# A graph network of four layers: the gate stage between layers 0 and 1 in a fixed order, its sums in memory

## The chip, the cores and the metric

The kernel runs on one core of a Trainium2 chip, in float32. Five engines take part, each with its own in-order queue of instructions: TensorE (PE; its weight loads are PEld), VectorE (DVE), ScalarE (ACT), GpSimd (POOL) and SyncE (SP, which here only issues DMAs; POOL issues DMAs too). The metric is the device time of one execution in microseconds (us). Before the change it is 2096.28 us, the median of 4 runs (2090.04 to 2102.93).

## The reference, cut to what matters

Eight graphs of 2048 nodes with 64 features go through four layers. Each adds its result to its input `x`. Two layers matter here:

```python
# layer 0, its end: every node mixes two candidates by a gate
pair  = stack([industry, g])                       # two vectors per node
coefs = softmax(tanh(pair @ fcW + fcb) @ av)       # over the two
x1    = x + coefs[0] * industry + coefs[1] * g
# layer 1, its start
h     = relu(layernorm(x1)) @ W                    # 'neighbours'
e     = leaky_relu(s_src[:, None] + s_dst[None])   # s = h @ a
x2    = x1 + elu(softmax(where(adj > 0.5, e)) @ h) # 'attention'
```

A softmax over two is a sigmoid of the difference of the scores, so the kernel computes `x1 = x + g + sigmoid(d) * (industry - g)`, where `sigmoid(d) = (1 + tanh(d / 2)) / 2`.

## The kernel before, in words

Two graphs share the 128 partitions, so there are four pairs p, and each pair's 2048 nodes are cut into four chunks c of 512 columns. All stages follow each other in one unrolled program, and a scheduler orders the instructions of each engine ahead of time by its own model. An instruction that goes through `tc.keep_in_program_order` is pinned: it is issued after the instruction that stands before it in the text on its engine. In the layers after the gate stage all matmuls are pinned (`kit.strict`, lines 711 to 721), other instructions are not.

Up to 437 us layer 0 has left `industry` of each chunk in device memory (`ind_dram`) and `g` of each pair on the chip (`gT`, the buffers `hn`). The second half of that (from 245 us, the "edge" stage, lines 1100 to 1187) also loads 12 of 16 tiles of the adjacency matrix (`aT`, 1 MB each) for layer 1. The last four (`aTl`) take the place of `gT[p]` when pair p is through (`late_tile`).

The **gate stage** (lines 1193 to 1264) runs over 16 chunks, pair by pair. For a chunk, `front` loads `industry` (buffer `iv`, 7 of them), puts it and `g` through `scores` (two matmuls into `pf`, a Tanh of 128x1024, L1206 and L1208), and takes two differences on DVE (L1217 of 128x1024, L1218 of 128x512). `back` runs two chunks behind: it multiplies the difference by `av` (`pd`, L1224), takes a Tanh (`cc`, L1226), does three DVE instructions of 128x512 (L1227 to L1229), of which the last adds `x`, which was loaded for it (`xo`, L1234), and writes the chunk to `x1_dram` with a DMA from POOL's queue (L1230).

Layer 1's first **neighbours** (`neighbour_steps(0)`, a generator) are advanced one or two steps per chunk from chunk 7 on. Per chunk of pair 0 it loads `x1` back from memory (L1302), then mean (PE), subtraction (DVE), Square (ACT), variance (PE), Ln and Exp (ACT), a DVE instruction, eight small matmuls `ph`, and copies to `hS`, `vd`, `sc`. At its end it computes the attention's row factors `R` for the first half of the nodes on the chip: 32 matmuls `pb` and four ACT copies (L1341 to L1346).

The **attention** of layer 1 (`attend`) follows. Its DVE instruction `pt` (L1387) makes the weights from `R` and a tile of the adjacency matrix, and PE multiplies them (`o`, `dn`). Its buffers (`att_pt`, six of 4 KB per partition) are opened once the gate stage's are closed, on the same side of the on-chip memory, so they lie where the small weights of layer 0, the `iv` buffers and part of the `th` buffers were.

Of the kernel before, what the change touches and what calls it, by code (L numbers as in the profile page):

```python
# [8 lines left out]
FP = mybir.dt.float32  # L9
FR = mybir.dt.float32r  # L10
AF = mybir.ActivationFunctionType
OP = mybir.AluOpType
# [4 lines left out]
P = 128  # L17
# [601 lines left out]
LN_EXP = "natural_log_exp_and_others"  # L619


class Kit:


# [124 lines left out]
def layer0(kit, hn, x1_dram, open_early, late_tile, between):  # L749
# [40 lines left out]
    with ExitStack() as sA:  # L790
# [110 lines left out]
        with ExitStack() as s1:  # L901
# [11 lines left out]
            def industry(c):  # L913

                acc = [ps.tile([P, CW], FP, tag=f"acc{p}", name=f"acc{p}") for p in range(NP)]
                ds = sb.tile([P, 2, CW], FR, tag="ds", name="ds")
                for g in range(NT // 2):
                    at = sp.tile([P, 2, CW], FR, tag="at", name="at")
                    nc.gpsimd.dma_start(
                        out=at,  # L920
                        in_=t["adjT"][g * 2 * P : (g + 1) * 2 * P, cols(c)].bitcast(FR).rearrange("(k p) n -> p k n", p=P),
                    )
                    for k in range(2):
                        m = 2 * g + k
                        for p in range(NP):
                            for h in range(2):
                                mm(acc[p], Y[h][:, m, p, :], at[:, k, :], start=m + h == 0, stop=m == NT - 1 and h == 1)  # L927
                        if units:
                            units.pop(0)()

                    if g > 0:
                        nc.vector.tensor_tensor(ds, (was if g == 1 else ds).bitcast(FP), at.bitcast(FP), op=OP.add)
                    was = at
                ev = [sb.tile([P, CW], FP, tag="ev", name="ev", bufs=4) for p in range(NP)]
                for p in range(NP):
                    (nc.scalar.copy if p % 2 else nc.vector.tensor_copy)(ev[p], acc[p])  # L936
                deg = ps.tile([P, CW], FP, tag="ph", name="deg", bufs=2)
                for k in range(2):
                    mm(deg, ones_r, ds[:, k, :], start=k == 0, stop=k == 1)
                rdeg = sb.tile([P, CW], FP, tag="rdeg", name="rdeg", bufs=1)  # L940
                nc.vector.tensor_reduce(bad[:, 3 + c : 4 + c], deg, AX.X, OP.min)
                nc.vector.tensor_scalar(bad[:, 3 + c : 4 + c], bad[:, 3 + c : 4 + c], 0.5, None, op0=OP.is_lt)
                nc.vector.tensor_scalar_max(rdeg, deg, 1.0)
                nc.vector.reciprocal(rdeg, rdeg)
                for p in range(NP):
                    nc.vector.tensor_mul(ev[p], ev[p], rdeg)
                    nc.sync.dma_start(out=ind_dram[p, :, cols(c)], in_=ev[p])
# [152 lines left out]
    with ExitStack() as s0:  # L1100
# [64 lines left out]
                nc.scalar.activation(gT[p][:, i * P : (i + 1) * P], pt[:, p, :], AF.Identity, bias=neg1)  # L1165

        now = begin(0)
        late = None
        for i in range(NT):
            pg = ps.tile([P, B, F], FP, tag="pg", name="pgs")  # L1170
# [16 lines left out]
        late()  # L1187

    sP.close()
    next_ = between(None)  # L1190


    with ExitStack() as s0:
        io = s0.enter_context(tc.tile_pool(name="o_io", bufs=7, reuse_waits="tile"))
        sb = s0.enter_context(tc.tile_pool(name="o_sb", bufs=2, reuse_waits="tile"))
        ps = s0.enter_context(tc.tile_pool(name="o_ps", bufs=2, space=PSUM, reuse_waits="tile"))

        def pinned(ins, first):

            if not first:  # L1200
                tc.keep_in_program_order(ins)

        def scores(v):
            pf = ps.tile([P, 2, CW], FP, tag="pf", name="pf")
            for b2 in range(2):
                pinned(mm(pf[:, b2, :], fcW[half(b2), :], v[half(b2), :], start=True, stop=True), b2 == 0)  # L1206
            th = sb.tile([P, 2, CW], FP, tag="th", name="th_s", bufs=4)
            nc.scalar.activation(th, pf, AF.Tanh, bias=fcb)  # L1208
            return th

        def front(p, c):
            s = cols(c)
            iv = io.tile([P, CW], FP, tag="iv", name="iv")
            nc.sync.dma_start(out=iv, in_=ind_dram[p, :, s])
            gv = gT[p][:, s]
            th = [scores(iv), scores(gv)]
            nc.vector.tensor_sub(th[0], th[0], th[1])  # L1217
            nc.vector.tensor_sub(iv, iv, gv)  # L1218
            return p, s, gv, th[0], iv

        def back(x, p, s, gv, th, df):
            pd = ps.tile([P, CW], FP, tag="pd", name="pd")
            for b2 in range(2):
                pinned(mm(pd[half(b2), :], Av, th[:, b2], start=True, stop=True), b2 == 0)  # L1224
            cc = sb.tile([P, CW], FP, tag="cc", name="cc", bufs=1)
            nc.scalar.activation(cc, pd, AF.Tanh, scale=0.5)  # L1226
            nc.vector.scalar_tensor_tensor(df, cc, 1.0, df, op0=OP.add, op1=OP.mult)  # L1227
            nc.vector.scalar_tensor_tensor(df, df, 0.5, gv, op0=OP.mult, op1=OP.add)
            nc.vector.tensor_add(x, x, df)  # L1229
            nc.gpsimd.dma_start(out=x1_dram[p, :, s], in_=x)  # L1230

        def inputs(p, c):
            x = sb.tile([P, CW], FP, tag="x", name="xo", bufs=5)
            nc.sync.dma_start(out=x, in_=t["xT"][p, :, cols(c)])  # L1234
            return x

        behind, freed, xs = [], [], []

        def finish():
            p, c, rest = behind.pop(0)  # L1240
            back(xs.pop(0), *rest)
            if freed:
                late_tile(freed.pop())
            if c == NCW - 1:
                freed.append(p)

        for p in range(NP):
            for c in range(NCW):
                behind.append((p, c, front(p, c)))
                if len(behind) > 1:  # L1250
                    xs.append(inputs(*behind[-2][0:2]))

                if NCW + 2 < p * NCW + c:
                    next(next_, None)
                if len(behind) > 2:
                    finish()
                if NCW + 2 < p * NCW + c:
                    next(next_, None)
        xs.append(inputs(*behind[-1][0:2]))
        for _ in next_:  # L1260
            pass
        while behind:
            finish()
        late_tile(freed.pop())
    ctx.close()


class Layer1:
# [19 lines left out]
    def neighbour_steps(self, p):  # L1288
# [3 lines left out]
        nc, mm = kit.nc, kit.mm  # L1292
        x1_dram, r_dram = self.x1_dram, self.r_dram

        keep = self.sb2 if p else sb
        sc = sb.tile([P, NT, 4], FP, tag="sc", name="sc", bufs=1)
        vd = keep.tile([P, NT, 2], FP, tag="vd", name="vd", bufs=1 + (p > 0))
        wd = keep.tile([P, NT, 2], FP, tag="wd", name="wd", bufs=1 + (p > 0))
        hS = None
        for c in range(NCW):  # L1300
            x = sb.tile([P, CW], FP, tag="x", name="x1", bufs=1)
# [27 lines left out]
        rs = sb.tile([P, 2, NT], FP, tag="rs", name="rs", bufs=1)  # L1329
        nc.scalar.activation(rs, sc[:, :, 2:4].rearrange("p t b -> p b t"), AF.Exp, scale=-0.8)  # L1330
        pr = ps.tile([2 * NT, P], FP, tag="h", name="pr")
        one = nc.tensor.transpose(pr, rs.rearrange("p b t -> p (b t)"), kit.ident)
        if kit.strict:
            kit.tc.keep_in_program_order(one)
        rr = sb.tile([2 * NT, P], FP, tag="rr", name="rr", bufs=1)
        nc.vector.tensor_copy(rr, pr)
        nc.sync.dma_start(out=r_dram[p].rearrange("b (t n) -> (b t) n", n=P), in_=rr)
        self.first = [self.scores(p, 0, b2) for b2 in range(2)] if p == 0 else None

        for b2, r in enumerate(self.first or ()):  # L1340
            for k in range(2):  # L1341
                pb = ps.tile([P, 4, P], FP, tag=("ln", "h")[k], name="pb1")
                for j in range(4):
                    one = rs[:, b2, 4 * k + j : 4 * k + j + 1]
                    mm(pb[:, j, :], one.to_broadcast([P, P]), kit.ident, start=True, stop=True)
                nc.scalar.copy(r[:, cols(k)], pb.rearrange("p k n -> p (k n)"))  # L1346
        yield hS, vd, wd

    def scores(self, p, hf, b2):

        self.turn += 1
        r = (self.sb2 if self.turn % 3 == 0 else self.R).tile([P, HN], FP, tag="R", name="R", bufs=2 - (self.turn % 3 == 0))
        if p == hf == 0:
            return r
        self.kit.nc.sync.dma_start(out=r, in_=self.r_dram[p, b2 : b2 + 1, cols(hf, HN)].to_broadcast([P, HN]))
        return r

# [57 lines left out]

        return [lambda: total(0), end]

    def run(self, aT, now, following):

# [4 lines left out]
        self.ps2 = l1.enter_context(tc.tile_pool(name="att_ps", bufs=2, space=PSUM, reuse_waits="tile"))  # L1426
        kit.use_ln_exp()
        kit.strict = True
        ends = []
        for p in range(NP):  # L1430
            last = p == NP - 1
            if last:
# [362 lines left out]
def four_layers(  # L1795
# [13 lines left out]
    with ExitStack() as s:  # L1809
# [18 lines left out]
            load(NT - NP + p, low.tile([P, N], FR, tag=f"hn{p}", name=f"aTl{p}"))  # L1828

        def between(_):  # L1830
            one = Layer1(kit, x1)
            ahead.append(one)

            def steps():
                for r in one.neighbour_steps(0):
                    yield
                ahead.append(r)

            return steps()

        layer0(kit, hn, x1, early, late_tile, between)
        later = []
# [2 lines left out]
            later.append(Layers23(kit, x1, x3, out, part, ctx))  # L1845
            return later[0].front(ps)

        ahead[0].run(aT, ahead[1], following)
        later[0].run(aT)
        ps = s.enter_context(tc.tile_pool(name="flag_ps", bufs=1, space=PSUM))  # L1850
        nc.vector.tensor_reduce(kit.bad[:, 0:1], kit.bad, AX.X, OP.add)
# [47 lines left out]
```

## Time and profile before

| what | value |
|---|---|
| median of 4 runs | 2096.28 us |
| the profiled execution | 2092.42 us, span 2090.6 us |
| PE busy | 2016.1 us (96%) |
| DVE, ACT, POOL busy | 1212.3 (58%), 461.6 (22%), 260.1 (12%) us |
| gate stage, first `pf` to first `pt` | 437.72 to 533.33 us |

The profile is a page of one execution: busy time of each engine, the span in 40 slices of 52.3 us with a digit for each engine's busy share and for the clock that TensorE was granted (PEclk), the chain of work that ended last, and the costliest groups of instructions. Other views answer for a stretch of time, a tile or a line: busy times by window, an engine's instructions in order of time, and who waited for whom. In a timeline row, the first number is the start, the second the length of the merged group, both in us, and brackets at the end give the idle time before it and what ended that. Instructions are named by line, operation, out<-in and count. A matmul in float32 shows as two instructions.

### The profile page before, as it was taken

What the parts mean: (1) busy time and instruction counts of PE and PEld (TensorE: products, weight loads), DVE (VectorE), ACT (ScalarE), POOL (GpSimd) and SP (SyncE); (2) the same over time, 40 slices, a digit from 0 to 9 for tenths busy, and PEclk for the clock granted to TensorE, in tenths of its full rate; (3) what the DMA queues carried; (4) which work ended last, traced back from release to release, by engine and by line L of the source; (5) the groups of instructions that cost most, each with busy time, mean ns of one, the idle gap of its engine ahead of it and who ended that gap; (6) DMA issues with size and microseconds to landing.
All of it is one profiled execution on the core that took longest, in us unless ns stands there. A gap on an engine that the chain in (4) does not pass through costs nothing.

```text
span 2090.6 us, 23652 instructions
## 1 busy us (share of the span) xinstructions
PE 2016.1 (96%) x9164; PEld 1153.2 (55%) x9164; DVE 1212.3 (58%) x1906; ACT 461.6 (22%) x863; POOL 260.1 (12%) x384
## 2 busy tenths in 40 slices
PE   7999898988999999999999999999999999999997
PEld 4777655622322222226776457765477755577653
DVE  6677488876888888884223652226642256522355
ACT  4321244456211111112121111211111211112100
POOL 0211054420000000000001110002100012100022
PEclk9999899998999999999999999999999999999999
DMA  5666272145111111213110012101022000121000
GB/s 129 184 194 194 76 255 57 37 133 169 62 41 41 42 41 26 61 31 87 57 41 20 24 28 66 56 11 31 22 61 60 30 21 25 37 66 55 6 15 12
DMA packets 85001, 136.06 MB, mean 65 GB/s; under 512 B 32912, under 2 KB 33168, under 8 KB 82640
## 3 DMA queue, kind: packets, MB, share of 16 engines
q1 hardware_dynamic: 66832, 83.86, 13.8%
q0 software_dynamic: 18048, 50.60, 8.8%
q8 instruction: 74, 1.21, 0.2%
q14 instruction: 47, 0.39, 0.1%
HBM read 103.69 MB, written 30.74 MB: 64 GB/s over the span
## 4 chain that ended last, share of the span: by engine, by line
PE 68%; issue 15%; DVE 6%; POOL 5%; DMA 3%; ACT 2%; SPq 0%; POOLq 0%; DVEq 0%; ACTq 0%
PE acc L713 27%; PE o L713 11%; PE dn L713 6%; PE u L713 6%; PE acc L927 2%; PE mean L713 2%; PE pgs L1155 2%; PE var L713 2%; PE py L713 2%; POOL fold L1780 1%; DVE ex L1153 1%; PE ph L713 1%; POOL ot L1781 1%; POOL mix L1154 1%; POOL ot L1782 1%
## 5 line engine op out<-in xcount | busy, mean ns | idle before, releaser
L713 PE MATMUL acc<-aT,parts 128*128 128x512 f32 x1664 | 456.0, 420 | 0.0
L713 PEld LDWEIGHTS acc<-aT,parts 128*128 128x128 f32 x1664 | 307.8, 188 | 111.8 <-issue 49.4
L1768 DVE TENSOR_TENSOR pr<-u,embf 128x512 f32<-128x512 f32 x256 | 170.7, 687 | 138.9 <-PE u L713 132.2
L1387 DVE SCALAR_TENSOR_TENSOR pt<-R,wd,aT 128x1024 f32<-128x1024 f32 x192 | 236.6, 1279 | 19.3 <-PE dn L713 8.1
L713 PE MATMUL o<-pt,hS 128*64 128x512 f32 x1024 | 237.8, 602 | 5.2 <-DVE pt L1387 5.1
L713 PE MATMUL u<-W3f,y 64*128 64x512 f32 x1024 | 241.0, 589 | 0.0
L713 PEld LDWEIGHTS u<-W3f,y 64*128 64x128 f32 x1024 | 99.2, 187 | 120.6 <-issue 120.6
L713 PEld LDWEIGHTS o<-pt,hS 128*64 128x64 f32 x1024 | 68.4, 137 | 165.0 <-issue 150.7
L713 PE MATMUL u<-W3f,v 64*128 64x512 f32 x512 | 138.8, 619 | 0.0
L927 PE MATMUL acc<-at,Y 128*128 128x512 f32 x512 | 134.9, 408 | 1.9 <-DVE ev L936 1.9
L713 PE MATMUL dn<-pt,vd 128*32 128x512 f32 x1024 | 123.1, 598 | 0.0
L1604 DVE TENSOR_TENSOR yb<-py,cb_f 128x512 f32<-128x512 f32 x32 | 22.1, 691 | 173.8 <-PE py L713 173.8
L1780 POOL TENSOR_TENSOR fold<-fold 128x256 f32<-128x256 f32 x64 | 47.7, 745 | 548.5 <-DVE fold L1779 510.6
L927 PEld LDWEIGHTS acc<-at,Y 128*128 128x128 f32 x512 | 93.9, 192 | 24.9 <-issue 4.2
L713 PE MATMUL acc<-aTl,parts 128*128 128x512 f32 x384 | 103.1, 405 | 0.0
L1772 DVE TENSOR_TENSOR pr<-pr 128x512 f32<-128x512 f32 x128 | 88.1, 688 | 2.2
L1387 DVE SCALAR_TENSOR_TENSOR pt<-R,wd,aTl 128x1024 f32<-128x1024 f32 x64 | 79.8, 1282 | 11.4 <-PE dn L713 8.2
L713 PEld LDWEIGHTS acc<-aTl,parts 128*128 128x128 f32 x384 | 72.2, 188 | 21.5 <-issue 5.7
L1155 PE MATMUL pgs<-mix,S 128*128 128x512 f32 x128 | 69.7, 635 | 12.8 <-POOL mix L1154 12.3
L1754 ACT COPY xs<-px 128x128 f32<-128x128 f32 x64 | 17.1, 267 | 272.7 <-POOL ot L1782 210.3
L1154 POOL TENSOR_TENSOR mix<-ex,wt 128x512 f32<-128x512 f32 x64 | 66.6, 1042 | 74.0 <-DVE ex L1153 64.0
L1672 POOL TENSOR_TENSOR bq<-bq,xp 128x512 f32<-128x512 f32 x16 | 20.5, 1283 | 434.1 <-DVE xp L1670 395.6
(307 smaller groups left out, 2711.0 us busy)
## 6 DMA issues: line engine op xcount, KB each, us to landing
at<-in_adjT POOLq DMA_DIRECT2D x32, 512.0 KB, 4.6
raw<-in_adjT SPq DMA_DIRECT2D x64, 256.0 KB, 3.4
aT<-in_adjT POOLq DMA_DIRECT2D x12, 1024.0 KB, 7.0
xp<-xd SPq DMA_DIRECT2D x45, 256.0 KB, 3.0
R<-r_dram SPq DMA_DIRECT2D x14, 512.0 KB, 3.9
hi_dram<-hi SPq DMA_DIRECT2D x16, 264.0 KB, 2.8
lo_dram<-lo SPq DMA_DIRECT2D x16, 264.0 KB, 3.4
hhi<-hi_dram POOLq DMA_DIRECT2D x16, 264.0 KB, 3.1
```

The costliest lines, as they stand in the source:

```text
L713: one = self.nc.tensor.matmul(*args, **kw)
L927: mm(acc[p], Y[h][:, m, p, :], at[:, k, :], start=m + h == 0, stop=m == NT - 1 and h == 1)
L1153: nc.vector.scalar_tensor_tensor(ex, mix, 1.0, ex, op0=OP.max, op1=OP.min)
L1154: nc.gpsimd.tensor_tensor(mix, ex, wt[:, k, :, None].to_broadcast([P, B, F]), op=OP.mult)
L1155: return lambda: mm(flat(pg), S[:, k, :], flat(mix), start=k == 0, stop=k == NB - 1)
L1387: nc.vector.scalar_tensor_tensor(pt, R[b2], wd[:, m, b2 : b2 + 1], aT[m][:, s].bitcast(FP), op0=OP.max, op1=OP.mult)
L1604: nc.vector.tensor_tensor(yb, py, bias[:, None, :].to_broadcast([P, 4, P]), op=OP.add)
L1768: nc.vector.tensor_tensor(a, u[h], emb[:, i, 8 * w : 8 * w + 8, None].to_broadcast([P, 8, F]), op=OP.mult)
L1772: nc.vector.tensor_add(pr[h], pr[h], a)
L1780: nc.gpsimd.tensor_add(fold[:, :, 0:2, :], fold[:, :, 0:2, :], fold[:, :, 2:4, :])
L1781: nc.gpsimd.tensor_add(ot, fold[:, :, 0, :], fold[:, :, 1, :])
L1782: nc.gpsimd.tensor_add(ot, ot, xs)
```

## The change

The gate stage is rewritten. Order: almost every instruction of PE, ACT and DVE in it goes through `keep_in_program_order` (the class `InOrder` does it for DVE and ACT), so the three engines run the text's order; DMAs stay free. Residual: `x` of pairs 1 to 3 is copied from the input to `x1_dram` by SP (1 MB each, memory to memory), issued in the text at the edge stage's start; `g` of these pairs is added to it by three adding DMAs of 1 MB from POOL's queue, and each chunk's own part by an adding DMA of 256 KB, instead of two DVE instructions, the load of `x` and the plain write. Pair 0 keeps its two additions and is written by SP. The factor 1/2 moves into `rdeg` (the industry is stored halved, its Tanh scales by 2). Neighbours: a new generator takes `x1` of pair 0 from the chip (`xs`, four buffers), two chunks at a time; `R` is no longer made on the chip but read back from memory as for later pairs, by two more loads of `R`.

```diff
-                nc.vector.tensor_scalar_max(rdeg, deg, 1.0)
+                nc.vector.tensor_scalar(rdeg, deg, 1.0, 2.0, op0=OP.max, op1=OP.mult)
...
         now = begin(0)
+        for p in range(1, NP):
+            nc.sync.dma_start(out=x1_dram[p], in_=t["xT"][p])
...
+        def scores(v, f):
+            act = A if kit.strict else nc.scalar
             pf = ps.tile([P, 2, CW], FP, tag="pf", name="pf")
             for b2 in range(2):
+                kit.strict = kit.strict or b2 == 1
+                mm(pf[:, b2, :], fcW[half(b2), :], v[half(b2), :], start=True, stop=True)
             th = sb.tile([P, 2, CW], FP, tag="th", name="th_s", bufs=4)
+            act.activation(th, pf, AF.Tanh, bias=fcb, scale=f)
+        def first(i):
+            p, c = chunks[i]
+            iv = ivs[i] = io.tile([P, CW], FP, tag="iv", name="iv")
+            nc.sync.dma_start(out=iv, in_=ind_dram[p, :, cols(c)])
+            ths[i] = scores(iv, 2.0)
+        def second(i):
+            p, c = chunks[i]
+            tgs[i] = scores(gT[p][:, cols(c)], 1.0)
+            V.scalar_tensor_tensor(ivs[i], gT[p][:, cols(c)], -0.5, ivs[i], op0=OP.mult, op1=OP.add)
+        def differ(i):
+            V.tensor_sub(ths[i], ths[i], tgs.pop(i))
+        def third(i):
+            for b2 in range(2):
+                mm(pd[half(b2), :], Av, th[:, b2], start=True, stop=True)
+            A.activation(ccs[i], pd, AF.Tanh, scale=0.5)
+        def fourth(i):
+            V.scalar_tensor_tensor(df, ccs.pop(i), 1.0, df, op0=OP.add, op1=OP.mult)
+            if p:
+                nc.gpsimd.dma_start(out=x1_dram[p, :, cols(c)], in_=df, accum_op=OP.add)
+            else:
+                V.tensor_add(df, df, gT[p][:, cols(c)])
+                V.tensor_add(xs[c], xs[c], df)
+                nc.sync.dma_start(out=x1_dram[p, :, cols(c)], in_=xs[c])
             if c == NCW - 1:
+                late_tile(p)
...
+        for p in range(1, NP):
+            nc.gpsimd.dma_start(out=x1_dram[p], in_=gT[p], accum_op=OP.add)
+        steps = one.first_neighbours(xs, V, A)
+        for i in range(len(chunks)):
+            if i > 2:
+                next(steps, None)
+            if 0 < i < len(chunks) - 1:
+                first(i + 1)
+            third(i)
+            if i + 1 < len(chunks):
+                second(i + 1)
+            fourth(i)
+            if i > 2:
+                next(steps, None)
+            if i + 1 < len(chunks):
+                differ(i + 1)
...
+    def first_neighbours(self, xs, V, A):
+        for d in (0, 2):
+            for k in range(2):
+                mm(mean, kit.avg, xs[d + k], start=True, stop=True)
+                V.tensor_sub(xc[k], xs[d + k], mean)
+                A.activation(q[k], xc[k], AF.Square)
+            yield
+            yield
+            for k in range(2):
+                mm(var[k], kit.avg, q[k], start=True, stop=True)
+            for k in range(2):
+                A.activation(q[k], var[k], AF.Ln, bias=kit.eps)
+            for k in range(2):
+                A.activation(q[k], q[k], AF.Exp, scale=-0.5)
+            yield
+            for k in range(2):
+                V.scalar_tensor_tensor(xc[k], xc[k], 0.0, q[k], op0=OP.max, op1=OP.mult)
+            yield
...
```

What is left out at the end: for each of the two chunks a step with the eight `ph` matmuls and two small Exp, and a step with the copies; then `wd` and `rs`, the transpose `pr`, the write of the row factors and the two loads of `R`. In `neighbour_steps`, now used for pairs 1 to 3 only, the on-chip `R` and its 32 matmuls are gone.

## The prediction, as put on record

> **What bounds it now.** The page has PE at 96% of the span, but only the gate stage changes, so I read that stage. First the windows by stage (columns: window, length, then busy us of PE, PEld, DVE, ACT and POOL, granted clock, DMA share, GB/s):
>
> ```profile
> 437.00:450.00 13.00, 12.64 (x44) 4.30 (x42) 6.57 (x8) 9.63 (x13) 0.00 (x0) 0.77 0.54 161
> 450.00:463.00 13.00, 12.24 (x48) 3.46 (x46) 12.86 (x19) 10.22 (x12) 2.24 (x5) 1.00 0.56 165
> 463.00:486.00 23.00, 15.00 (x34) 4.39 (x32) 11.01 (x17) 9.41 (x12) 1.61 (x3) 0.73 0.61 193
> 486.00:523.00 37.00, 33.78 (x116) 11.83 (x116) 29.72 (x52) 30.38 (x41) 4.33 (x8) 0.98 0.52 171
> 523.00:534.00 11.00, 7.61 (x43) 4.44 (x39) 8.64 (x14) 6.34 (x11) 2.29 (x5) 1.00 0.29 101
> ```
>
> Three regimes: DVE full (450 to 463), a hole with no engine full (463 to 486), then PE, DVE and ACT all near 0.8 to 0.9. What the hole is, the chain of waits says:
>
> ```profile
> 462.99 9.25 DMA xd<-xo
> ...
> 472.67 4.75 DMA x<-xd
> 477.42 0.14 issue
> 477.56 2.04 PE mean L713 x2
> ```
>
> The chunk of `x1` goes to memory behind a 1 MB `aTl` load and comes back, and PE, whose order is fixed, waits at `mean`. The end (523 to 534) is a third loss: `pb` and the copies to `R` stand before the first `pt` at 533.33. So the stage takes 95.6 us (437.72 to 533.33), and no engine is its bound throughout.
>
> **What goes.** DVE: for 12 chunks two of four 128x512 instructions, 24 of 0.69 (L1228, L1229) = 16.5 us. ACT: loads of the function table fall from 8 to 4 of 1.28 = 5.1 us; four copies to `R`, 2.3. PE: 32 `pb`, 4.0. The round trip of `x1` (14 us of chain) goes. SP loses 12 `xo` and 4 `x1` loads, POOL 16 writes. These are large, but they count only as far as the new order lets the engines use them.
>
> **What the order costs.** In the text, chunk i runs: `pd(i)`, second scores of i+1, its Tanh, the difference of i+1 on DVE, and only then `pd(i+1)`. On PE `pd(i+1)` stands ahead of the next second scores, so this is a loop, one round per chunk, with no chunk of slack; before, `back` ran two chunks behind. The links, from these rows (start, length in us):
>
> ```profile
> 450.32 1.13 PE L1206 MATMUL pf<-iv,fcWf 64*128 64x512 f32 x4
> 451.29 1.02 PE L1206 MATMUL pf<-hn,fcWf 64*128 64x512 f32 x4
> 451.50 2.38 ACT L1208 ACTIVATE th_s<-pf,fcbf 128x1024 f32<-128x1024 f32 x2 [0.32 <-PE pf L1206]
> ...
> 495.65 1.10 ACT L1208 ACTIVATE th_s<-pf,fcbf 128x1024 f32<-128x1024 f32 x1
> 496.79 1.23 DVE L1217 TENSOR_TENSOR th_s<-th_s 128x1024 f32<-128x1024 f32 x1 [0.31 <-ACT th_s L1208]
> ```
>
> A four-matmul group holds PE for 1.0 us; from the start of a `pf` group to its Tanh are 1.18 (450.32 to 451.50), the Tanh lasts 1.10, the difference starts 0.04 later and lasts 1.22, and a hop from DVE to PE is 0.1 (`gn` ends 436.56, `ptg` starts 436.70). Round: 1.0 + 1.18 + 1.1 + 0.04 + 1.22 + 0.1 = **4.64 us**. The first scores of the next chunk fit into its gap of 1.6. Before, groups of three (two `pf`, one `pd`) came every 2.93 us, then 3.66 once DVE was full: the order costs more than DVE did.
>
> - Pair 0 keeps three DVE instructions after `cc`, ahead of the difference: 1.2 (`pd` to `cc`) + 0.6 + 3 x 0.7 + 1.22 + 0.15 = 5.27 per round.
> - Start: the first three score groups run at half clock as now (437.72, 439.59, 441.29); the third is now `g`'s, so its Tanh starts at 443.2, the difference ends 445.5, `pd(0)` starts at 445.6.
> - 15 rounds: 4 x 5.27 + 11 x 4.64 = 72.1.
> - A round with two means: difference 1.22, two subtractions 1.32, last Square 0.63, Tanh 1.11, `cc` 0.6, Tanh 1.11 = 6.0, so +1.4; twice, 2.8.
> - A round with two Ln: ACT runs table load, two Ln, load, two Exp, then Tanh, `cc`, Tanh: 2 x 1.28 + 2 x 0.69 + 2 x 0.62 + 1.11 + 0.6 + 1.11 = 8.0, and DVE puts `df` and two 0.66 instructions ahead of the difference, 8.9: +4.3; twice, 8.6.
> - Four rounds with copies (0.16 + 0.41 twice on DVE, of which 0.9 fits in a gap): +0.25 each, 1.0.
> - End after `pd(15)` starts: 1.2 + 0.6 + 0.7 = 2.5.
>
> 445.6 + 72.1 + 2.8 + 8.6 + 1.0 + 2.5 = 532.6 against the 533.4 at which `xo` now ends. **At full clock the order gives back all that was saved.**
>
> **The clock.** Windows around the start of the stage (same columns):
>
> ```profile
> 430.00:435.00 5.00, 2.75 (x4) 0.80 (x4) 2.27 (x3) 0.72 (x1) 2.08 (x2) 0.76 0.16 59
> 435.00:440.00 5.00, 4.12 (x11) 1.90 (x12) 0.85 (x2) 1.29 (x5) 0.00 (x0) 0.50 0.53 157
> 440.00:445.00 5.00, 4.64 (x16) 1.35 (x12) 2.37 (x3) 3.91 (x4) 0.00 (x0) 0.71 0.86 260
> 445.00:450.00 5.00, 5.00 (x24) 1.39 (x20) 4.05 (x5) 4.42 (x6) 0.00 (x0) 1.00 0.01 5
> ```
>
> PE idled for 0.59 and 2.19 us (428 to 432), then the clock is halved until PE has been full for some us. At 5 us windows of 3.0 to 3.7 busy the clock held (65:70, 245:250), so a normal round, 3.0 of 4.64, should hold. In each Ln round PE waits some 3.2 us (two `var`, `pf`, `pd`, `pf` are through 5.1 us into it; `ph` needs the first of DVE's two instructions: 6.9 for `cc`, + 0.7 + 0.7 = 8.3), and at the start PE waits for the first difference. Estimate: after an Ln round a group each of `ph` (1.3), `pf`, `pd` (1.0 each) runs at half clock, up to +3.3, I take 2.8, twice; 1.0 at the start: **+6.6**. Bounds: 0, and half clock in all rounds, +2.0 each, about +26 more.
>
> The Trainium skill ("TensorE: Matmul & The Clock Gate", section "Why this matters for your kernels") only warns of idle gaps over about 3 us between bursts. The row disagrees: 2.19 us was the longest gap before this fall. By the rule the start would cost nothing and the Ln gaps are on its edge, so the stage could end at 532.6; by the row it is 6.6 later.
>
> **The rest.** The three 1 MB copies by SP stand near 250 us, beside `aT` loads. The edge stage had PE busy 45.15 of 50 us at DMA share 0.73 (250:300) and 45.00 at 0.23 (350:400), so it hides DMA: 0, at most +3. An adding DMA of 512 KB took 5.6 us to landing (`xd<-e`) and 0.84 of POOL. Three of 1 MB from 439 are two such each: some 30 us, over before pair 1's attention input is read. Behind them on POOL's queue stand only the chunks' adds and `aTl`; aTl's last use begins 37 us after the stage (570.53). The `iv` buffer is now held until its add has landed, but seven buffers at 4.64 give 28 us. The two `R` loads (3.9) follow the neighbours' last step, chunk 11, four rounds before the end: hidden. Halving in `rdeg`: same instruction, 0. What is open is the first `pt`: its buffers lie where the last `iv` were. Free at once: -2.8 (PE need not wait from the last `pd` to the first `pt`); after the last add: 0.84 + 5.6 = +6.4. I take +1, since only some of six buffers are held.
>
> **Sum.** -0.8 + 6.6 + 1.0 = +6.8 on the profiled execution, 2092.4 to 2099.2. That execution lies 3.9 under the median, so 2096.3 + 6.8 = **2103 us**. A change under 0.5% (10.5 us) is about what this measurement can't tell from none.
>
> **Rivals.**
> 1. *The loop isn't closed, the fullest engine sets the pace.* PE: 16 x 3.0 + 4 x (2.1 + 1.3) = 62, with start and end (7.9 + 2.5) 72 instead of 95.6: -23, 2073. For it: all three engines lose work, PE had 0.94 in 450:463. Against: the text above. Chance 0.15.
> 2. *Full clock, and free `pt` instructions fill DVE's gaps before the end.* -0.8 - 2.8: 2093, 0.10.
> 3. *Slower: the clock doesn't come back.* Place: the gaps of the strict loop; price +2.0 per round beyond those counted. From two further rounds on it is over +10.5; with half of the rounds, +13 to 16 more: 2118. For it: 480:485 still had 0.50 with PE at 5.00. Against: at half clock PE is 6.0 of 6.7 full. Chance 0.22.
> 4. *Attention's start waits for the last adding DMA*: +5.4 over the forecast, 2108.5, 0.13.
>
> That the change doesn't do what it says can only be so in part, as DMAs are free to move.
>
> **Chances.** Forecast 0.40, rivals 0.15, 0.10, 0.22, 0.13. Faster by over 0.5%: rival 1 and 0.02 of the others, 0.17. Slower: rival 3, most of 4, a part of the forecast's own spread, 0.37. Between: 0.46. Range: rival 1 (0.15) and rival 3's far end are left out, 2084 to 2121.
>
> **What would show it.** Right: between 450 and 530 no engine over 0.8 busy; `pd` every 4.6 to 5.3 us, with two rounds of some 9; PE's waits ended by the difference (L1217's successor), clock under 1 after each Ln; no wait of `mean` for a DMA. Wrong: `pd` every 3 to 3.7 us (rival 1), or clock 0.5 through most of the stage (3), or PE idle over 4 us at the first `o` (4). A stage end before 520 would refute the loop.

## The result, and the profile after

The kernel after takes **2100.26 us** (median of 52 runs, 2093.73 to 2111.23) against 2095.71 (78 runs of the kernel before, 2086.8 to 2104.4): a ratio of 1.0027, with a 95% interval of 1.0019 to 1.0035. The two medians by themselves are 4.55 us apart; the differences below go by the ratios, so it is slower by 5.7 us (0.0027 x 2095.7), less than 0.5%. The forecast was +6.8. The profiled execution took 2099.19 us with a span of 2097.4. PE is busy for 2010.3 us (before 2016.1), DVE for 1198.4 (1212.3), ACT for 455.8 (461.6): all three do less, and the time is longer.

From here on, "the stage" is the time from the first `pf` to the first `o` in one trace: 96.95 us before (437.72 to 534.67), **102.30** after (436.70 to 539.00), so +5.35. In the kernel's new text the pinned DVE and ACT instructions all have line L630 (the helper `InOrder`), pinned matmuls L726, `pt` L1465, a chunk's adding DMA L1258, the 1 MB ones L1275.

The windows by stage of the kernel after, in the same stretches and columns as those of before:

```profile
437.00:450.00 13.00, 9.82 (x24) 2.88 (x22) 5.51 (x7) 6.65 (x10) 2.67 (x3) 0.67 0.87 171
450.00:463.00 13.00, 10.54 (x32) 2.76 (x32) 9.36 (x14) 5.54 (x8) 0.00 (x0) 0.87 0.71 191
463.00:486.00 23.00, 17.50 (x62) 6.47 (x60) 11.73 (x19) 15.63 (x22) 2.28 (x3) 0.85 0.46 103
486.00:523.00 37.00, 28.33 (x103) 9.81 (x101) 20.80 (x36) 23.77 (x33) 6.22 (x8) 0.91 0.66 135
523.00:534.00 11.00, 5.52 (x22) 1.39 (x20) 6.09 (x7) 6.12 (x7) 3.11 (x4) 1.00 0.72 150
```

From 450 on no engine is over 0.81 busy, and in the last stretch PE, DVE and ACT are all near half: nothing is full, so something waits in a circle. The chain of waits shows the circle in a plain round (start, length, what):

```profile
515.78 1.08 PE pd L726 x4
516.86 1.08 PE pf L726 x4
...
517.96 1.12 ACT th_s L630
...
519.11 1.24 DVE th_s L630
...
520.39 1.08 PE pd L726 x4
```

`pd`, second scores, Tanh, difference, next `pd`: 4.61 us, five times in a row, against 4.64 predicted. A round with Ln in it, from the same view:

```profile
466.04 1.28 ACT L630
...
467.34 1.27 ACT q L630 x2
...
469.92 1.15 ACT q L630 x2
471.06 1.00 ACT th_s L630
472.07 0.50 ACT cc L630
...
472.59 0.69 DVE iv L630
473.28 0.61 DVE xc L630
...
474.03 2.10 PE ph L726 x8
476.12 2.01 PE pf L726 x4
478.13 1.78 PE pd L726 x4
```

ACT loads a table, makes two Ln, loads again, makes two Exp; the text then sends a Tanh and `cc` through ACT and `df` through DVE before DVE may make `xc`, for which PE waits. And `ph`, `pf` and `pd` then take twice their length, which the windows confirm (column 8 is the granted clock):

```profile
475.00:480.00 5.00, 5.00 (x16) 1.81 (x16) 1.31 (x2) 1.53 (x4) 0.00 (x0) 0.54 0.54 68
480.00:485.00 5.00, 4.13 (x22) 1.64 (x20) 3.42 (x7) 2.94 (x5) 0.87 (x1) 1.00 0.36 67
```

At the end, DVE's rows in order of time:

```profile
536.88 0.69 DVE L630 SCALAR_TENSOR_TENSOR iv<-cc,iv 128x512 f32<-128x512 f32 x1 [2.71 <-ACT cc L630]
537.57 3.67 DVE L1465 SCALAR_TENSOR_TENSOR pt<-R,wd,aT 128x1024 f32<-128x1024 f32 x3
543.92 3.68 DVE L1465 SCALAR_TENSOR_TENSOR pt<-R,wd,aT 128x1024 f32<-128x1024 f32 x3 [2.68 <-DMA xd<-iv]
```

The first three `pt` start at once; the fourth waits 2.68 us for an adding DMA, because, as the trace's releaser and e5_swap below say, its buffer lies on an `iv` buffer that the DMA still reads.

### The profile page after: what moved, and what is told of

It reads as the page before. It is cut to its first block, busy times and chain, and to the rows that moved or that the text cites. A ratio compares the mean times of both kernels' runs of the same rounds, so it can differ in the third digit from the quotient of the medians.

```text
span 2097.4 us, 23519 instructions
## 1 busy us (share of the span) xinstructions
PE 2010.3 (96%) x9132; PEld 1150.8 (55%) x9132; DVE 1198.4 (57%) x1882; ACT 455.8 (22%) x855; POOL 264.7 (13%) x383
## 4 chain that ended last, share of the span: by engine, by line
PE 68%; issue 15%; DVE 6%; POOL 5%; ACT 2%; DMA 2%; POOLq 0%; DVEq 0%; SPq 0%; ACTq 0%
PE acc L726 27%; PE o L726 11%; PE dn L726 6%; PE u L726 6%; PE acc L940 2%; PE pgs L1169 2%; PE mean L726 2%; PE var L726 2%; PE py L726 2%; POOL fold L1858 1%; DVE ex L1167 1%; PE pf L726 1%; PE ph L726 1%; POOL ot L1859 1%; POOL ot L1860 1%
## 5 line engine op out<-in xcount | busy, mean ns | idle before, releaser
L726 PE MATMUL acc<-aT,parts 128*128 128x512 f32 x1664 | 455.7, 419 | 0.0
L726 PEld LDWEIGHTS acc<-aT,parts 128*128 128x128 f32 x1664 | 307.7, 188 | 111.7 <-issue 49.4
L1465 DVE SCALAR_TENSOR_TENSOR pt<-R,wd,aT 128x1024 f32<-128x1024 f32 x192 | 236.5, 1279 | 20.6 <-PE dn L726 6.6
L726 PE MATMUL o<-pt,hS 128*64 128x512 f32 x1024 | 238.2, 602 | 4.3 <-DVE pt L1465 4.1
L726 PE MATMUL u<-W3f,y 64*128 64x512 f32 x1024 | 241.0, 589 | 0.0
L726 PEld LDWEIGHTS u<-W3f,y 64*128 64x128 f32 x1024 | 99.2, 187 | 120.6 <-issue 120.6
L726 PEld LDWEIGHTS o<-pt,hS 128*64 128x64 f32 x1024 | 68.6, 137 | 164.6 <-issue 154.5
L726 PE MATMUL u<-W3f,v 64*128 64x512 f32 x512 | 138.8, 619 | 0.0
L726 PE MATMUL dn<-pt,vd 128*32 128x512 f32 x1024 | 123.1, 598 | 0.0
L726 PE MATMUL acc<-aTl,parts 128*128 128x512 f32 x384 | 103.2, 405 | 0.0
L1465 DVE SCALAR_TENSOR_TENSOR pt<-R,wd,aTl 128x1024 f32<-128x1024 f32 x64 | 79.8, 1281 | 11.4 <-PE dn L726 8.2
L726 PEld LDWEIGHTS acc<-aTl,parts 128*128 128x128 f32 x384 | 72.2, 188 | 21.6 <-issue 5.7
```

Source lines behind the costliest of these rows:

```text
L726: one = self.nc.tensor.matmul(*args, **kw)
L1465: nc.vector.scalar_tensor_tensor(pt, R[b2], wd[:, m, b2 : b2 + 1], aT[m][:, s].bitcast(FP), op0=OP.max, op1=OP.mult)
```

## The experiments

All ratios are against the kernel before, measured beside the kernel on the same chip. "Stage" is from each kernel's own trace. "Plain round" is the distance of `pd` in rounds that hold no work of the neighbours. The profiled execution of e1_slack was its fastest (2095.81 us), that of e5_swap its slowest (2099.24).

| kernel | what differs | stage, us | plain round, us | ratio (95% interval) |
|---|---|---|---|---|
| before | | 96.95 | 2.92 to 3.49 | 1 |
| after | | 102.30 | 4.61 | 1.0027 (1.0019 to 1.0035) |
| e1_slack | a chunk of slack in the text | 102.32 | 2.93 | 1.0058 (1.0041 to 1.0076) |
| e2_free | order left to the scheduler | 85.40 | 4.60 | 0.9959 (0.994 to 0.9978) |
| e3_fill | PE's gaps filled | 94.19 | 4.61 | 0.9998 (0.9986 to 1.0009) |
| e4_dve_sum | residual undone | 114.87 | 5.09 to 6.27 | 1.01 (1.0083 to 1.0116) |
| e5_swap | e1, `pt` not on `iv` | 97.95 | 2.93 | 1.0008 (0.9993 to 1.0023) |
| e6_memory | neighbours undone | 122.50 | 4.61 | 1.0121 (1.0101 to 1.014) |
| e7_free_dve | e2, residual undone | 86.87 | 2.07 to 5.73 | 0.9955 (0.9942 to 0.9969) |
| e8_early | e5, `xc` earlier | 76.74 | 2.93 | 0.9915 (0.9896 to 0.9933) |
| e9_early_dve | e8, residual undone | 87.42 | 3.8 | 0.9964 (0.995 to 0.9977) |
| e10_early_fill | e8, gaps filled | 74.77 | 2.93 | 0.9906 (0.9883 to 0.9928) |
| e11_sooner | e10, neighbours one chunk sooner | 77.20 | 2.93 | 0.9915 (0.99 to 0.9929) |

The time that lies outside the stage (median less stage) is 1998.8 us before, 1998.0 after, and between 1996.3 and 1999.8 in every other row but e1_slack (2002.9). So, to within some 3 us, the stage is where every one of these edits acts.

**e1_slack.** Does the order close the loop?

```diff
-            third(i)
             if i + 1 < len(chunks):
                 second(i + 1)
-            fourth(i)
-            if i > 2:
-                next(steps, None)
+            third(i)
             if i + 1 < len(chunks):
                 differ(i + 1)
+            fourth(i)
+            if i > 2:
+                next(steps, None)
```

> One move in the text: the second scores of chunk i+1 stand before pd of chunk i, and its difference before fourth of chunk i. Theory (the strict order closes a loop of 4.6 us, second scores, Tanh, difference, pd): the loop now has a chunk of slack, pd comes every 3.0 to 3.3 us in plain rounds, every 4.1 in pair 0 (DVE: 1.22 + 4 x 0.69), rounds with two Ln take some 8 (ACT's own work). Stage from first pf to first o 78 us instead of 102; time 2075 us (2070 to 2082). Rival (DMA traffic or buffers that come free late set the pace, the order only happens to fit it): rounds stay above 4.3, time 2093 or more.

Measured: 1.0058, 3 permille above the change. The loop did open; the matmuls of its last chunks, and then the first `o`:

```profile
517.36 1.08 PE L726 MATMUL pd<-th_s,Avf 128*64 128x512 f32 x4
...
520.29 1.08 PE L726 MATMUL pd<-th_s,Avf 128*64 128x512 f32 x4
...
523.22 1.08 PE L726 MATMUL pd<-th_s,Avf 128*64 128x512 f32 x4
525.91 1.08 PE L726 MATMUL pd<-th_s,Avf 128*64 128x512 f32 x4 [1.61 <-DVE th_s L630]
537.09 3.87 PE L726 MATMUL o<-pt,hS 128*64 128x512 f32 x8 [10.10 <-DVE pt L1465]
```

2.93 us per chunk, PE without a gap up to the last `pd`, and then 10.10 us of nothing. So the closed loop is shown, but its rate alone was not worth the 25 us expected: the stage is as long as before. Two other places took it back: the rounds with Ln grew from 9.67 and 10.30 to 13.92 and 11.82 us, and the first `pt`, which came at once in the change, waited:

```profile
526.75 8.67 DMA xd<-iv
...
535.65 1.29 DVE pt L1465
```

The adding DMA was issued at 526.75 on POOL's queue, 2.1 us after a 1 MB load of `aTl` (524.69), and landed 8.67 us later. That is rival 4 of the prediction, in full size, in a kernel that reaches the place sooner.

**e5_swap.** The same with the two pools in the other order, so that `pt` lies on `th`, `cc` and `x`:

```diff
-        io = s0.enter_context(tc.tile_pool(name="o_io", bufs=7, reuse_waits="tile"))
         sb = s0.enter_context(tc.tile_pool(name="o_sb", bufs=2, reuse_waits="tile"))
+        io = s0.enter_context(tc.tile_pool(name="o_io", bufs=7, reuse_waits="tile"))
```

> e1_slack with two lines changed places: the pool of th, cc and x is opened before the pool of iv, so that the attention's pt buffers lie over th, cc and x and not over the iv buffers, which the adding DMAs hold. Theory (e1_slack opened the loop, and the first pt then waited 7.3 us for an adding DMA, more in its timed runs): pt starts within 2 us of the last pd, first o at 529 to 530 in the trace instead of 537.1, time 2087 (2083 to 2091). Rival (e1_slack loses its time by DMA traffic in the whole stage, and the wait at its end is only where it shows): 2096 or more.

Measured: 1.0008, 10 us below e1_slack (0.0050 x 2094) but less than expected. In its trace the wait is gone (last `pd` 535.41, first `pt` 537.77), and the stage is only 4.4 us shorter, because its two rounds around the first Ln were 0.63 and 1.62 us longer than in e1_slack, with both `pf` at half clock, and its first `pd` came 1.13 us later after the stage's start. The rest of the 10 us lies outside the stage, in e1_slack's 2002.9. The rounds with Ln, 14.55 and 11.45 us, are now by far the longest.

**e8_early.** The neighbours' second step goes ahead of the next difference and of `fourth`:

```diff
             third(i)
+            if i > 2:
+                next(steps, None)
             if i + 1 < len(chunks):
                 differ(i + 1)
             fourth(i)
-            if i > 2:
-                next(steps, None)
```

> e5_swap with the second step of the neighbours ahead of the next difference and of fourth in the text (as it stands in the change). Theory (in e1_slack ph waited 7.7 and 5.8 us because DVE's instruction for xc stood behind the difference and fourth, and these behind two Tanh and cc on ACT): ph comes 3 us earlier in each Ln round, the clock falls less: 2080 (2075 to 2085). Rival (the Ln round is ACT's own 8 us, wherever xc stands): within 2 us of e5_swap.

Measured: 0.9915, 2075.82 us, inside the expectation. PE's rows around the first Ln, e1_slack and then e8_early:

```profile
458.41 1.08 PE L726 MATMUL pd<-th_s,Avf 128*64 128x512 f32 x4
467.21 2.10 PE L726 MATMUL ph<-W1x,xc 128*128 128x132 f32 x8 [7.72 <-DVE xc L630]
```

```profile
468.62 1.08 PE L726 MATMUL pd<-th_s,Avf 128*64 128x512 f32 x4
473.06 1.17 PE L726 MATMUL ph<-W1x,xc 128*128 128x132 f32 x8 [3.37 <-DVE xc L630]
```

The wait for `xc` falls from 7.72 to 3.37 us. Against e5_swap, whose waits for `xc` are the same 7.72 and 5.77 us as in e1_slack, the place of one step in the text was worth 19 us (0.0093 x 2092). This kernel is faster than the one before and the one after, and computes the same. DVE's rows at the end of its stage:

```profile
519.68 0.69 DVE L630 SCALAR_TENSOR_TENSOR iv<-cc,iv 128x512 f32<-128x512 f32 x1 [1.21 <-ACT cc L630]
520.29 1.28 DVE L1465 SCALAR_TENSOR_TENSOR pt<-R,wd,aT 128x1024 f32<-128x1024 f32 x1
521.74 3.68 DVE L1465 SCALAR_TENSOR_TENSOR pt<-R,wd,aT 128x1024 f32<-128x1024 f32 x3 [0.17 <-DMA R<-r_dram]
```

The first `pt` follows straight behind the last `fourth`, and the first `o` (521.71) behind this `pt`. Only the second `pt` waits for its half of R, whose load took 8.06 us, and DVE loses no more than 0.17 us by it.

**e2_free.** Order of DVE and ACT free; of the gate's matmuls only the second of each pair pinned; the rest of the change stays.

```diff
-    V, A = InOrder(tc, nc.vector), InOrder(tc, nc.scalar)
+    V, A = nc.vector, nc.scalar
...
-    mm = kit.mm
+    def mm(*args, **kw):
+        one = nc.tensor.matmul(*args, **kw)
+        if pair.pop():
+            tc.keep_in_program_order(one)
+
+    pair = [True, False] * 100
```

> Order of the gate stage left to the scheduler again: DVE and ACT free, and of the gate's matmuls only the second of each pair pinned, as before the change; neighbours' matmuls stay pinned, residual and neighbours as in the change. Theory: rounds without a neighbours' matmul gain slack and fall toward 3.5, rounds with one keep theirs; 5 to 12 us less, 2088 to 2095. Rival (order not at fault): 2098 to 2102, rounds unchanged.

Measured: 0.9959, 14 us below the change (0.0068 x 2094), where 5 to 12 were expected: the change's residual and neighbours with the scheduler's order are faster than the kernel before. The reason in the expectation was wrong: the plain rounds stayed at 4.60, since the scheduler kept `pd` ahead of the second half of the second scores there, for which the Tanh waits. The rounds with neighbours shrank: the nine from `pd(2)` to `pd(11)` take 44.9 us (457.39 to 502.26) against 60.3 (455.46 to 515.78). DVE's rows of e2_free show why:

```profile
469.23 1.29 DVE L1398 SCALAR_TENSOR_TENSOR xc<-xc,q 128x512 f32<-128x512 f32 x2 [1.65 <-ACT q L1395]
471.24 0.69 DVE L1261 SCALAR_TENSOR_TENSOR iv<-cc,iv 128x512 f32<-128x512 f32 x1 [0.71 <-ACT cc L1256]
```

`xc` stands ahead of `df` and starts as soon as its Exp is there. `ph` then waits 0.80 and 1.82 us instead of 3.50 and 4.12, and the clock does not fall in either Ln round.

**e3_fill.** What does the clock cost? Matmuls whose result is overwritten fill PE's gaps, for example:

```diff
             th = ths.pop(i)
+            for k in range(8 if i == 15 else 4 if i < 4 else 0):
+                mm(pd[:, 0:P], kit.ident, kit.ident, start=True, stop=True)
```

and in the same way 16 ahead of the first `ph` after each Ln, and 8 ahead of the first `o`.

> Extra matmuls whose results are overwritten fill PE's gaps: 4 ahead of pd in chunks 0 to 3, 8 ahead of the last pd, 16 ahead of the first ph after each Ln, 8 ahead of the first o. Nothing else changes. Theory (half clock after the gaps costs some 6 to 8 us on the path): granted clock stays 1 after both Ln rounds and at the first o, ph x8 takes 1.1 instead of 2.1, the round after it 4.6 to 5 instead of 5.9, o x8 2.4 shorter; time 2092 to 2095. Rival (the clock falls beside the path, the Ln rounds are long by ACT and DVE alone): no more than 2 us less, or some us more where the fill itself delays pd.

Measured: 0.9998, 6.1 us below the change (0.0029 x 2094), inside the expectation. PE's rows around the first Ln:

```profile
471.88 3.84 PE L726 MATMUL ph<-ident_f 128*128 128x128 f32 x32
475.56 1.07 PE L726 MATMUL ph<-W1x,xc 128*128 128x132 f32 x8
476.55 1.13 PE L726 MATMUL pf<-iv,fcWf 64*128 64x512 f32 x4
477.61 1.08 PE L726 MATMUL pd<-th_s,Avf 128*64 128x512 f32 x4
```

`ph` takes 1.07 instead of 2.10, `pf` 1.13 for 2.08, `pd` 1.08 for 1.82, with more work on PE and not less. From `pd(0)` to `pd(15)` this kernel needs 82.4 us, the change 89.6: 7.2 us.

**e4_dve_sum.** Only the residual undone.

```diff
-            if p:
-                nc.gpsimd.dma_start(out=x1_dram[p, :, cols(c)], in_=df, accum_op=OP.add)
-            else:
-                V.tensor_add(df, df, gT[p][:, cols(c)])
-                V.tensor_add(xs[c], xs[c], df)
-                nc.sync.dma_start(out=x1_dram[p, :, cols(c)], in_=xs[c])
+            x = xs[c] if p == 0 else more.pop(i)
+            V.tensor_add(df, df, gT[p][:, cols(c)])
+            V.tensor_add(x, x, df)
+            (nc.gpsimd if p else nc.sync).dma_start(out=x1_dram[p, :, cols(c)], in_=x)
```

> Only the residual undone: no copies of x in memory, no adding DMAs; pairs 1 to 3 load x, add g and x with two DVE instructions per chunk and write plainly, as pair 0 does. Order and neighbours as in the change. Theory: the two additions stand ahead of the next difference on DVE and lengthen the loop by 0.5 to 0.7 in 12 rounds, 1.4 at the end: 2107 to 2110. Rival (memory traffic of the adding DMAs costs time elsewhere, or the first pt waits for them): the same as the change or up to 3 us faster, 2097 to 2101.

Measured: 1.01, 15 us above the change (0.0073 x 2094), where 7 to 10 were expected: the last five rounds are 5.90, 5.71, 5.09, 6.27 and 5.09 us, 1.0 over 4.61 in the mean, not 0.5 to 0.7. In the chain of waits the two additions stand in the loop, and a longer gap on PE halves the clock (`pd` 1.80 and `pf` 2.02):

```profile
534.29 0.70 DVE iv L630
...
535.62 1.23 DVE th_s L630
...
536.89 1.80 PE pd L726 x4
538.69 2.02 PE pf L726 x4
```

**e7_free_dve** and **e9_early_dve** undo the residual in the same way in two other orders: in that of e2_free, and in that of e8_early.

> e2_free with the residual undone as in e4_dve_sum (x loaded, g and x added by DVE in all pairs, plain writes). Theory (the additions cost only because they stand in the strict loop; 0.6 per round there): against e2_free 4 to 8 us more, 2089 to 2093, the last pt no longer held by an adding DMA (-3). Rival (the residual in memory is worth as much in any order as the 14 us between the change and e4_dve_sum): 2097 or more.

> e8_early with the residual undone as in e4_dve_sum. The two additions were worth 14 us in the strict loop of the change and nothing (2084.0 against 2084.7 us) in the scheduler's order. Theory (DVE paces where the order has slack: 1.22 + 4 x 0.69 = 4.0 per chunk against PE's 2.93): plain rounds 4.0 to 4.1, 8 to 12 us more than e8_early, 2084 to 2088. Rival (the adding DMAs' traffic takes as much back): within 3 us of e8_early.

Measured: e7_free_dve has 0.9955 against 0.9959 of e2_free, no difference, and both numbers of its expectation missed. e9_early_dve has 0.9964 against 0.9915 of e8_early, 10 us, as expected. Its plain rounds are 3.8 us where e8_early has 2.93, with DVE busy for 19.66 of the 20 us from 500: there DVE is what paces. A further 2.46 us is a wait of its last addition for the load of `x`. In e7_free_dve the rounds alternate (2.79, 5.73, 2.07, 5.55), 16.1 us for four where e2_free needs 18.4: the scheduler made another order of it, so this pair compares two orders as well as two residuals. The same edit is worth 15, 0 or 10 us, by the order it stands in.

e7_free_dve shows one thing more. What it keeps of the change is the neighbours by the chip and the text in which they stand; the sums in memory and the pinned DVE and ACT are gone. It is 9 us below the kernel before (0.0045 x 2092). So what the change won in the scheduler's order came with the neighbours and their text, not with the residual.

**e6_memory.** Only the neighbours undone: `x1` of pair 0 read back, one chunk at a time, by the generator of the later pairs.

```diff
-        steps = one.first_neighbours(xs, V, A)
+        steps = one.from_memory()
...
+    def from_memory(self):
+        for r in self.neighbour_steps(0):
+            yield
+        self.first = [self.scores(0, 0, b2) for b2 in range(2)]
+        self.now = r
```

> Only the neighbours undone: the gate stage in the strict order and with the adding DMAs, but x1 of pair 0 read back from memory, one chunk at a time, by the generator of the later pairs (its DVE and ACT instructions not pinned), R still read back. Theory (two chunks at a time make two rounds of 10 us, out of the strict order they would not): four Ln rounds of 6 to 8 us in place of two of 10, clock falls less, 2092 to 2101. Rival (the way by the chip is what keeps the stage as short as it is, the round trip of x1 comes back as in the kernel before): 2105 or more.

Measured: 1.0121, 20 us above the change (0.0094 x 2092). The theory's 2092 to 2101 missed; the rival's number (2105 or more) came, but its reason only in small part. PE's rows:

```profile
461.06 2.08 PE L726 MATMUL mean<-x,avg_f 128*128 128x512 f32 x2 [3.88 <-DMA x<-xd]
...
485.23 1.12 PE L726 MATMUL var<-q,avg_f 128*128 128x512 f32 x2
491.28 1.22 PE L726 MATMUL ph<-W1x,xc 128*128 128x132 f32 x4 [4.92 <-DVE xc L754]
```

Only one `mean` waits for the memory (3.88 us). The rest is that in this generator `ph` follows straight behind `var` on PE, so that the whole way over Ln, Exp and `xc` lies open, four times (4.83 to 4.92 us). This run therefore does not tell what the way by the chip is worth; it points to what the empty steps of the new generator, which put `pf`, `pd` and `pf` between `var` and `ph`, are worth, but does not separate them from the rest that differs (one chunk at a time, DVE and ACT not pinned).

**e10_early_fill** and **e11_sooner.** e8_early with 10 filling matmuls ahead of the first `ph` after each Ln, 5 ahead of the last `pd`, 8 ahead of the first `o`; and this with the neighbours begun one chunk sooner.

```diff
+                    for j in range(10 if k == g == 0 else 0):
+                        mm(ph[:, 0, 0:P], kit.ident, kit.ident, start=True, stop=True)
```

```diff
-            if i > 2:
+            if i > 1:
```

> e8_early with extra matmuls whose results are overwritten: 10 ahead of the first ph after each Ln, 5 ahead of the last pd, 8 ahead of the first o. Theory (half clock costs what its share of the work costs): ph, pf and o that ran at half clock at 474 to 478, 495 to 499 and 522 to 526 run at full clock, 3 to 5 us less, 2071 to 2073. Rival (the waits behind, for R and ACT, take it up): within 1.5 us of e8_early.

> e10_early_fill with the neighbours' steps begun one chunk earlier (i > 1 for i > 2). In e8_early the first o waited for R, whose way through memory took 5.4 and 8.1 us after the neighbours' end. Theory: R is there 3 us earlier, first pt straight after the last fourth; 1 to 3 us less than e10_early_fill. Rival (the mean then waits for the x1 of chunk 1, and the round where DVE is full takes it back): the same or more.

Measured: 2074.57 and 2076.04 us beside 2075.82 of e8_early; the intervals overlap, and neither is told apart from it. In the traces the fill shortens the stage by 2.0 us and the clock no longer falls after its start. In e11_sooner no `pt` waits for R any more. But the first `o` had not waited for R, as the expectation says it did: the second `pt` had, for 0.17 us in e8_early and 0.47 in e10_early_fill, so there was little to win; and the round with the first means takes 9.34 us instead of 4.86, as the rival said.

**e12_slack_again.** e1_slack once more.

> e1_slack once more, one look: its trace (first pf to first o 102.3 us, as in the change) does not account for a median 5 us above the change. Theory (the first pt's wait for the adding DMA varies and was short in that trace): the wait is 12 us or more in this trace, the time 2100 or more. Rival (the time goes elsewhere): the same wait of 7 to 8 us at a time over 2100.

Measured: 2107.22 us, stage 101.93, first `pt` again held for 7.28 us. The theory falls and its rival holds: the time is not in the stage. The first `pf` starts at 444.72 here and at 434.77 in e1_slack, 10 us apart in two executions of one kernel. Half of this is there by 40 us (a DMA that POOL issues at 37.70 in e1_slack comes at 42.55 here); the other half comes between 255 and 273 (POOL's `mix`, 254.93 against 260.37, and a few instructions on 262.94 against 272.98). A row from the first place and the window around the second, e1_slack and then e12_slack_again:

```profile
24.09 3.78 PE L857 MATMUL pr<-tri,MT 64*128 64x64 f32 x32 [1.33 <-DVE Y L905]
...
260.00:280.00 20.00, 17.13 (x78) 11.20 (x78) 17.50 (x27) 8.69 (x19) 11.38 (x15) 1.00 0.74 257
```

```profile
26.13 6.38 PE L857 MATMUL pr<-tri,MT 64*128 64x64 f32 x32 [1.34 <-DVE Y L905]
...
260.00:280.00 20.00, 17.67 (x66) 11.76 (x65) 12.68 (x19) 6.46 (x16) 9.27 (x12) 0.77 0.60 199
```

The same 32 matmul rows take 6.38 us for 3.78, and around 270 PE is as busy at a clock of 0.77 for 1.00 and does 66 rows instead of 78. So the clock is behind the 10 us between these two executions. It does not explain why e1_slack's median stands 3 us over its stage plus 2000; that stays open, and since the interval of its ratio reaches 3.7 us to either side, it may be no more than scatter.

## Why the prediction was right

By its own steps:

- **The loop.** Predicted 4.64 us per plain round, measured 4.61; `pd(0)` 7.9 us after the stage's start, measured 7.96 (444.66 - 436.70). e1_slack shows that it is the order: with a chunk of slack the round is 2.93. Rival 1 ("the fullest engine sets the pace", stage 72 us, 2073) was wrong for this kernel, and near for the one with slack and `xc` in its place: 75.32 us from the first `pf` to the first `pt`, 2075.8, with PE busy for all of the 16 us from 500.
- **Rounds with neighbours.** Predicted from `pd(0)` to `pd(15)` at full clock 72.1 + 2.8 + 8.6 + 1.0 = 84.5; e3_fill, at full clock, needs 82.4. The two Ln steps were predicted as ACT's and DVE's own 8.9 us in one round; in the change they spread over two (6.24 and 9.67, 5.04 and 10.30).
- **The clock.** Predicted 6.6 us; filling the gaps gave 6.1 in time and 7.2 between the first and last `pd`. This is the term that decided the sign: without it the sum is -0.8 + 1.0. That the two Ln rounds would halve the clock and that it would come back (no rival 3) is as predicted. Not foreseen: a fall in pair 0 (`pd` at 455.46 takes 1.78, behind gaps of 1.07 and 2.09 us), and one at the end, after the gap of 2.48 us ahead of `pd(15)`, where no first scores are left to fill PE.
- **The rule that was weighed.** The Trainium skill ("TensorE: Matmul & The Clock Gate", section "Why this matters for your kernels") asks for no idle gaps over about 3 us. The row of 534.23 disagrees again: idle 2.48 us ahead of it, `pd` 1.98 instead of 1.08, `o` x8 4.78 us. But the length of a gap alone does not decide: the last `pd` of e2_free, behind 2.46 us, took 1.08, and `ph` of e8_early, behind 3.37 us, took 1.17; the rows behind them are slow. Four rounds of 4.61 in a row, with gaps of 1.62, 1.20, 1.62 and 1.62 us, kept the full clock.
- **The first `pt`.** Taken at +1, with -2.8 and +6.4 as bounds. Measured: the first came at once, the fourth waited 2.68 us, and the lag behind the kernel before grew from 4.33 us at the first `o` to 5.07 at the first `pt` of `aTl` (575.60 against 570.53): 0.74. Rival 4 named the right place; e1_slack shows its full price, 7.3 us of DVE, as soon as the last chunks come faster.
- **The copies by SP** were costed at nothing, "near 250 us". They were issued at 42.65, so the place was wrong. The price holds to within the scatter of some 3 us: e4, e7 and e9, which have no copies, show 1999.1, 1997.1 and 1998.7 us outside the stage, the others 1996.3 to 1999.8 (e1_slack apart). The three 1 MB adding DMAs, put at some 30 us, landed within 16.8 us of their issue.
- **What goes.** The prediction counted DVE's 16.5 us and the round trip as given, and said that they count only as far as the order lets the engines use them. e4_dve_sum puts the first at 15 us in this order. So the sum of +6.8 hides large terms of both signs: about -15 for the residual, and +14 for the order against the scheduler's (e2_free), in which the clock's 6 are contained. They are not independent: in the scheduler's orders, e2_free beside e7_free_dve, the residual shows no gain.
- **Luck.** The sum gives 101.5 us from the first `pf` to the first `pt` (532.6 + 6.6 - 437.72); the trace has 100.87 (537.57 - 436.70). It is this near because errors cancel: the rounds at full clock were put 2.1 us too long, the clock between the first and the last `pd` 0.6 too short, and the end after `pd(15)` 0.8 too short (2.5 for 3.34, with `pd` at half clock).

## What to carry to other kernels

Before pinning an order, follow one result round the engines and back: if it needs its own predecessor's last step, its links add up, however idle each engine is. A chunk of slack opens such a loop, but the time it frees can go to the next wait, as it did here. Then look at what stands behind each rare long step (here two Ln and two Exp) on every in-order queue: moving one step of the neighbours ahead of the DVE instructions that waited for ACT was worth 19 us on top of the slack, the slack by itself nothing; the move without the slack was not run. A buffer that a DMA still reads should not lie under the first tile of the next stage.

## What the runs showed of the hardware

- In all 14 traces the granted clock changes on a grid of 3.41 us. From 400 to 545 us it halved 53 times, each time after a stretch of this grid in which PE had been busy for 0.46 of the time or less; the stretches behind which the full clock stayed had 0.45 or more. So in this stage it is the busy share of a stretch that goes with a fall, not the longest gap. The plain rounds of the change are just above this share, 1.80 of 3.42, the last one, which has no first scores, below it:

```profile
527.39:530.81 3.42, 1.80 (x10) 0.38 (x8) 1.89 (x3) 1.99 (x3) 0.85 (x1) 1.00 1.04 225
530.81:534.22 3.41, 0.95 (x4) 0.12 (x3) 1.92 (x2) 1.65 (x2) 1.41 (x2) 1.00 0.34 35
534.22:537.63 3.41, 1.98 (x4) 0.29 (x4) 0.75 (x2) 1.36 (x2) 0.00 (x0) 0.50 0.95 173
```

- Extra matmuls in the gaps won 6 us in the change, and nothing that can be told apart in e8_early.
- A 256 KB adding DMA landed after a median of 5.0 us in the change; one that was issued 2.1 us behind a 1 MB load on the same queue took 8.67. The three 1 MB adding DMAs took a median of 11.8.
- The stretch ahead of the stage differed by 10 us between two executions of the same kernel, about half of it with the clock in 260:280 at 1.00 and at 0.77. A few us are therefore read from a stage inside a trace, or from medians of many runs, not from two profiled times.
